# Perceiver layer: the routing between attention and the experts, rewritten around one root, one rank step and a gather by token tiles

## The chip, the cores and the metric

The kernel runs on one core of one Trainium2 chip. The metric is device time in microseconds (us) of one execution. Between changes of this kernel it is the median of several runs.

## The reference

One transformer-like layer over 256 tokens of width 512, in float32, with a context of 25088 rows. It adds three blocks to x, each behind a layernorm: a two-way cross attention with the context, a self-attention with 16 heads, and a feed-forward block with a shared expert and 32 routed ones, of which each token goes to one. Only the last block matters here:

```python
x = x + _L0_ffn_ref(_layernorm(x), gate_w, shared_gate_w, ..., routed_down_w)
# inside, x is the normalized input of 256 tokens:
shared_out = silu(x @ sg) * (x @ su) @ sd
logits = x @ gate_w                            # 32 experts
topk_ids = argmax(logits, -1); topk_val = max(logits, -1)
xs = x * sigmoid(topk_val)[:, None]
order = argsort(topk_ids); sorted_x = xs[order]
g = ragged_dot(sorted_x, routed_gate_w, tokens_per_expert)
u = ragged_dot(sorted_x, routed_up_w, tokens_per_expert)
d = ragged_dot(silu(g) * u, routed_down_w, tokens_per_expert)
return shared_out + d[argsort(order)]
```

Gate, up and down matrices are 512x1024, 512x1024 and 1024x512 for each expert, 2 MB each: 96 matrices, 192 MB (of 2 MB = 2097152 bytes), are read once.

## The kernel before

The 256 tokens are two token tiles (t = 0, 1) of 128 partitions. Matrix products are on TensorE (PE), each product of float32 appearing in the trace as two records; vector work on VectorE (DVE); activations and half of the copies out of PSUM on ScalarE (ACT); transfers are issued by SyncE's queue (SP), in order. The program runs under a tile framework that puts in the waits between engines and may order instructions on an engine; the changed kernel uses its `issue_after` to say behind which instruction another one is to stand.

Stages, by the profile's clock: the cross attention over 49 blocks of 512 context rows until about 690 us, its gate and mix until 724, self-attention until 808, routing until 822, experts until the end. There are 11 slots of 2 MB for weights (`feed`, `done`, lines 118 to 129): a list names the matrices to come in order, and when the last reader of a slot is through, SP may issue the next transfer into it (line 122). At the start of the routing gate (rg), up (ru) and down (rd) of experts 0 to 2 and some more are in the slots or on their way.

Routing, lines 779 to 835, before the change, with the names that the rows use:

- y[t] in PSUM holds the sum behind self-attention (line 745 is its last product). Each tile has statistics (788), mean and variance (184), variance plus eps (ve, 186), a square root on ACT (188), a reciprocal (190) and the normalization into h2: tile 0 on DVE (196), tile 1 on ACT (194).
- Four PE transposes for each tile give h2T (792), copied out by DVE or ACT (101/99). ACT also copies y[t] to x_sb (835), from which a product with the identity opens the output's sum acc[t] (969), written in the loop behind expert 0's products but placed on PE among the transposes.
- Logits lg (798), eight records for each tile; then on DVE the maximum mx (803), a comparison (805), a sum with `far` (807), a minimum that gives the expert's number eid (808), and the one-hot row (809).
- The rank of a token within its expert: products with `before` (a strict triangle) and, for tile 1, with `ones` (817, 818); then a product with the one-hot row, a sum and key = 256*eid + rank (820, 822, 823).
- The score is a sigmoid (829), and h2 is scaled by it on ACT (831).
- `select(g)` (841) compares the keys with the slots of four experts at a time (32 slots for each expert), and `gather_tokens` multiplies h2 with that selection (884): four column chunks c, the two token tiles within each. `spread_keys` (854) puts all keys in every partition, `count_more` (866) counts tokens above 32 for an expert.
- Experts: `expert_up` (902) makes gate and up products, `expert_down` (921, 930) the down products and their sum into acc through a selection. Shared expert work (940, 952) is spread over experts 3 to 12.

Of the kernel before, what the change touches and what calls it, by code (L numbers as in the profile page):

```python
# [48 lines left out]
def perceiver_layer(  # L49
# [45 lines left out]
    def evacuate(dst, src):  # L95

        turn[0] ^= 1
        if turn[0]:
            nc.vector.tensor_copy(dst, src)  # L99
        else:  # L100
            nc.scalar.copy(dst, src)  # L101


    x_sb = keep.tile([P, NT, H], F32, tag="x", name="x_sb")
    nc.sync.dma_start(x_sb, x)
# [22 lines left out]
    def done(name):  # L128
        feed(weights.pop(name)[1])

    def feed_pair(slot, name, src):
# [4 lines left out]
        for k in range(2):  # L136
# [26 lines left out]
    )  # L163
    iota_m = cpool.tile([P, P], F32, tag="iota_m", name="iota_m")
    nc.gpsimd.iota(iota_m, pattern=[[1, P]], base=0, channel_multiplier=0,
                   allow_small_or_imprecise_dtypes=True)

    iota_4 = cpool.tile([P, P], F32, tag="iota_4", name="iota_4")
# [12 lines left out]
    def normalize(dst, src, stats, name, on_scalar=False):  # L181

        mv = small.tile([P, 2], F32, tag="ln_mv", name=f"{name}_mv")
        nc.vector.bn_aggr(mv, stats)
        ve = small.tile([P, 1], F32, tag="ln_ve", name=f"{name}_ve")
        nc.vector.tensor_scalar(ve, mv[:, 1:2], EPS, None, ALU.add)
        sd = small.tile([P, 1], F32, tag="ln_sd", name=f"{name}_sd")
        nc.scalar.activation(sd, ve, AF.Sqrt)
        rs = small.tile([P, 1], F32, tag="ln_rs", name=f"{name}_rs")
        nc.vector.reciprocal(rs, sd)  # L190
        if on_scalar:
            off = small.tile([P, 1], F32, tag="ln_off", name=f"{name}_off")
            nc.vector.tensor_scalar(off, mv[:, 0:1], rs, -1.0, ALU.mult, ALU.mult)
            nc.scalar.activation(dst, src, AF.Identity, bias=off, scale=rs)
        else:
            nc.vector.tensor_scalar(dst, src, mv[:, 0:1], rs, ALU.subtract, ALU.mult)
# [439 lines left out]
    with tc.tile_pool(name="att", bufs=1, reuse_waits="tile") as at:  # L636
# [117 lines left out]
        for hp in range(HC):  # L754
# [10 lines left out]
                att_out(hp - 1, last)  # L765
            pr = following
        att_out(HC - 1, oh)
        done("w_o")
        at_stack.close()

# [11 lines left out]
    eid = fp.tile([P, NT], F32, tag="eid", name="eid")  # L782
    onehot = fp.tile([P, NT, E], F32, tag="onehot", name="onehot")
    far = fp.tile([P, E], F32, tag="far", name="far")
    nc.vector.tensor_scalar(far, iota_m[:, :E], float(E), None, ALU.add)
    for t in range(NT):
        st = small.tile([P, 6], F32, tag="ln_st", name=f"ln2_st{t}")
        nc.vector.bn_stats(st, y[t])
        normalize(h2[:, t, :], y[t], st, f"ln2_{t}", on_scalar=(t == 1))
        pt = tr_bank(f"h2T_{t}")  # L790
        for c in range(KC):
            nc.tensor.transpose(pt[:, ts(c, P)], h2[:, t, ts(c, P)], ident)
        evacuate(h2T[:, :, ts(t, P)], pt.rearrange("p (c n) -> p c n", c=KC))
    mx = fp.tile([P, NT], F32, tag="mx", name="mx")
    for t in range(NT):
        pm = tr_bank(f"lg_{t}")
        for c in range(KC):
            nc.tensor.matmul(
                pm[:, :E], h2T[:, c, ts(t, P)], gw_sb[:, c, :],
                start=(c == 0), stop=(c == KC - 1),  # L800
            )

        nc.vector.tensor_reduce(mx[:, t : t + 1], pm[:, :E], AX.X, ALU.max)
        cand = small.tile([P, E], F32, tag="cand", name=f"cand_{t}")
        nc.vector.tensor_scalar(cand, pm[:, :E], mx[:, t : t + 1], -float(E),
                                ALU.is_equal, ALU.mult)
        nc.vector.tensor_tensor(cand, cand, far, ALU.add)
        nc.vector.tensor_reduce(eid[:, t : t + 1], cand, AX.X, ALU.min)
        nc.vector.tensor_scalar(
            onehot[:, t, :], iota_m[:, :E], eid[:, t : t + 1], None, ALU.is_equal  # L810
        )


    for t in range(NT):
        pm = tr_bank(f"rank_{t}")
        for k in range(t):
            nc.tensor.matmul(pm[:, :E], ones, onehot[:, k, :], start=(k == 0), stop=False)
        nc.tensor.matmul(pm[:, :E], before, onehot[:, t, :], start=(t == 0), stop=True)
        rk = small.tile([P, E], F32, tag="cand", name=f"rk_{t}")
        nc.vector.tensor_tensor(rk, onehot[:, t, :], pm[:, :E], ALU.mult)  # L820
        rank = small.tile([P, 1], F32, tag="rank", name=f"rank_{t}")
        nc.vector.tensor_reduce(rank, rk, AX.X, ALU.add)
        nc.vector.scalar_tensor_tensor(
            key[:, t : t + 1], eid[:, t : t + 1], float(N), rank, ALU.mult, ALU.add
        )


    score_sb = fp.tile([P, NT], F32, tag="score", name="score_sb")
    nc.scalar.activation(score_sb, mx, AF.Sigmoid)
    for t in range(NT):  # L830
        nc.scalar.activation(
            h2[:, t, :], h2[:, t, :], AF.Copy, scale=score_sb[:, t : t + 1]
        )
    for t in range(NT):
        nc.scalar.copy(x_sb[:, t, :], y[t])

    def select(g):

        sl = fp2.tile([P, NT, P], F32, tag="sel", name=f"sel_{g}", bufs=1)
        for t in range(NT):  # L840
            nc.vector.tensor_scalar(
                sl[:, t, :], iota_4, float(4 * N * g), key[:, t : t + 1], ALU.add, ALU.is_equal
            )
        return sl

    keys = fp.tile([P, N], F32, tag="keys", name="keys")

    def spread_keys():

        pm = tr_bank("keys")  # L850
        for t in range(NT):
            dg = fp2.tile([P, P], F32, tag="selT", name=f"dg_{t}")
            nc.vector.tensor_scalar(dg, ident, key[:, t : t + 1], None, ALU.mult)
            nc.tensor.matmul(pm[:, ts(t, P)], ones, dg, start=True, stop=True)
        nc.vector.tensor_copy(keys, pm[:, :N])
# [23 lines left out]
    def gather_tokens(name, sels):  # L879

        pt = tr_bank(f"xg_{name}")
        for c in range(KC):
            for t in range(NT):
                nc.tensor.matmul(
                    pt[:, ts(c, P)], h2[:, t, ts(c, P)], sels[:, t, :],
                    start=(t == 0), stop=(t == NT - 1),
                )
        xg = fp2.tile([P, KC, P], F32, tag="xg", name=f"xg_{name}", bufs=1)
        for half in range(2):
            evacuate(  # L890
                xg[:, 2 * half : 2 * half + 2, :].rearrange("p c m -> p (c m)"),
                pt[:, ts(half, 2 * P)],
            )
        return xg

    def expert_up(name, xg, j, wg_e, wu_e):

# [31 lines left out]
        for t in range(NT):  # L929
            nc.tensor.matmul(accs[t], slT[:, ts(t, P)], d, start=start, stop=stop)  # L930

    acc = [acc_bank(f"acc_{t}") for t in range(NT)]

    def shared_hidden(i):

        w = weight(f"sh_{i // 4}", IC // 2 * P)
# [22 lines left out]
    for e in range(E):  # L959
        wg_e, wu_e = weight(f"rg_{e}", I), weight(f"ru_{e}", I)  # L960
        g, j = divmod(e, 4)
        if j == 0:
            xg = gather_tokens(str(g), select(g))
        act = expert_up(str(e), xg, j, wg_e, wu_e)
        done(f"rg_{e}")
        done(f"ru_{e}")
        if e == 0:
            for t in range(NT):
                nc.tensor.matmul(acc[t], ident, x_sb[:, t, :], start=True, stop=False)

            shT = keep.tile([P, 4, N], F32, tag="x", name="shT")
            spread_keys()
        elif e == 1:
            count_more()
        if pending is not None:
            expert_down(*pending)
            done(f"rd_{e - 1}")
        if 5 <= e < 5 + IC:
            shared_out(e - 5)
        if 3 <= e < 3 + IC:  # L980
            shared_hidden(e - 3)
# [13 lines left out]
    with tc.If(any_more > 0):  # L995
        for s in range(MORE):
# [38 lines left out]
            for t in range(NT):  # L1035
                kr = small.tile([P, 1], F32, tag="o_kr", name=f"o_kr_{s}_{t}")
                nc.vector.tensor_tensor(kr, key[:, t : t + 1], k0, ALU.subtract)
                nc.vector.tensor_scalar(
                    sl[:, t, :CAP], iota_m[:, :CAP], kr, None, ALU.is_equal
                )  # L1040
            xg = gather_tokens(f"o{s}", sl)
# [81 lines left out]
```

## Time and profile before

| | |
|---|---|
| median of 3 runs | 1273.73 us (1271.55 to 1274.98) |
| profiled execution, its time | 1273.0 us |
| its span, first to last instruction | 1271.0 us |
| mean granted TensorE clock | 0.974 |
| busy PE / DVE / ACT / POOL | 1142.1 / 567.3 / 217.4 / 199.2 us |
| read from HBM | 328.82 MB |
| the chain of waits, by engine | PE 70%, DMA 25%, DVE 3%, issue 1%, ACT 1% |

How to read the rows below. A timeline row has the start in us from the span's start, the length, the engine, the line, the operation, output<-inputs and shapes, how many instructions were merged (x), and, in brackets, the idle time of the engine before it and what ended it. A row of a window has the stretch, its length, busy time of PE, PE's weight loads, DVE, ACT and POOL with numbers of instructions, the granted PE clock (1.00 is full speed), the busy share of the DMA engines and GB/s. A row of the chain has start, length, engine, output and line. Ends of matmuls are modelled.

### The profile page before, as it was taken

The page shows a single profiled execution, that of the slowest core. Times are in us where ns is not written, and L with a number is a line of the kernel's source. Part 1 is how long each engine was busy: PE and PEld are TensorE (multiplying, and loading weights), DVE is VectorE, ACT ScalarE, POOL GpSimd, SP SyncE. Part 2 cuts the span into 40 slices and gives each one's busy share as a digit, 9 for nine tenths or more (in the row PEclk, how much of TensorE's full clock was granted, in tenths as well). Part 3 has the DMA queues.
Part 4 walks back from the last instruction along what each step waited for, and adds up shares of the span by engine and source line. Part 5 has one row for each costly group of instructions (what it writes and reads, how often), then busy time and mean ns, then how long its engine had stood idle before and what let it go on. Part 6 is the DMA issues. An engine that isn't in the chain of part 4 may idle for free.

```text
span 1271.0 us, 16289 instructions
## 1 busy us (share of the span) xinstructions
PE 1142.1 (90%) x6732; PEld 833.5 (66%) x6732; DVE 567.3 (45%) x1078; ACT 217.4 (17%) x457; POOL 199.2 (16%) x166
## 2 busy tenths in 40 slices
PE   7999999999999999999999999899998767566665
PEld 6788888888888888888887666554544223222321
DVE  2267766876667866668766445511111010010000
ACT  0222221222211222212221233310001000000000
POOL 1015313333123332133331000000000000000000
PEclk9999999999999999999999999999999898998898
DMA  9554444445444444444441480699999999999996
GB/s 387 228 198 166 166 166 149 163 163 187 151 154 160 166 166 166 166 146 165 163 154 36 181 348 15 259 419 430 430 430 428 430 428 432 429 429 429 429 430 260
DMA packets 30894, 330.44 MB, mean 260 GB/s; under 512 B 3553, under 2 KB 3681, under 8 KB 4065
## 3 DMA queue, kind: packets, MB, share of 16 engines
q1 hardware_dynamic: 30816, 329.36, 65.3%
q8 instruction: 55, 0.90, 0.3%
q14 instruction: 23, 0.18, 0.0%
HBM read 328.82 MB, written 0.52 MB: 259 GB/s over the span
## 4 chain that ended last, share of the span: by engine, by line
PE 70%; DMA 25%; DVE 3%; issue 1%; ACT 1%; POOL 0%; DVEq 0%; ACTq 0%; SPq 0%
PE sc L392 26%; PE p L514 22%; DMA rd<-in_ro_d_dram 9%; DMA rg<-in_ro_g_dram 9%; DMA ru<-in_ro_u_dram 6%; PE d L921 2%; PE rg L902 2%; PE acc L930 2%; PE ru L902 2%; PE y L745 1%; PE vh L654 1%; PE shg L940 1%; PE q L676 1%; PE shu L940 1%; PE k L676 1%
## 5 line engine op out<-in xcount | busy, mean ns | idle before, releaser
L392 PE MATMUL sc<-aT,ctxT 128*128 128x256 f32 x1568 | 341.3, 380 | 0.8 <-DMA ctxT<-in_cxT_dram 0.8
L392 PEld LDWEIGHTS sc<-aT,ctxT 128*128 128x128 f32 x1568 | 298.6, 191 | 40.8 <-ACT st L396 1.1
L514 PE MATMUL p<-diffs,sums 128*128 128x256 f32 x576 | 156.0, 380 | 0.4 <-DVE diffs L480 0.4
L514 PEld LDWEIGHTS p<-diffs,sums 128*128 128x128 f32 x576 | 109.6, 190 | 15.3 <-DVE diffs L480 0.8
L921 PE MATMUL d<-rd,actT 128*32 128x512 f32 x512 | 77.2, 717 | 37.8 <-DMA rd<-in_ro_d_dram 29.5
L396 ACT COPY st<-sc 128x512 f32<-128x512 f32 x98 | 57.3, 585 | 277.7 <-PE sc L392 277.7
L442 POOL TENSOR_TENSOR ls<-ls,st 128x512 f32<-128x512 f32 x64 | 104.2, 1628 | 3.8
L902 PE MATMUL ru<-ru,xg 128*32 128x256 f32 x1024 | 68.7, 407 | 37.8 <-DMA ru<-in_ro_u_dram 37.8
L400 DVE TENSOR_TENSOR mx<-mx,st 128x512 f32<-128x512 f32 x64 | 47.0, 734 | 124.4 <-ACT st L396 124.0
L514 PE MATMUL p<-ctx,st 128*128 128x256 f32 x384 | 98.6, 380 | 0.0
L928 DVE TENSOR_SCALAR selT<-keys,slot_key 128x256 f32<-128x256 f32 x32 | 11.2, 353 | 179.4 <-PE acc L930 179.4
L908 DVE TENSOR_TENSOR act<-act,ru 128x256 f32<-128x256 f32 x32 | 13.5, 421 | 165.7 <-PE ru L902 165.7
L930 PE MATMUL acc<-d,selT 128*128 128x512 f32 x128 | 66.5, 643 | 16.5 <-ACT d L101 16.5
L514 PEld LDWEIGHTS p<-ctx,st 128*128 128x128 f32 x384 | 73.1, 190 | 9.7
L902 PEld LDWEIGHTS ru<-ru,xg 128*32 128x32 f32 x1024 | 32.9, 116 | 70.3 <-DMA ru<-in_ro_u_dram 46.9
L409 POOL PARTITION_ALL_REDUCE mbc<-mx x17 | 18.8, 1104 | 361.1 <-DVE mx L401 353.9
L438 ACT ACTIVATE st<-st 128x512 f32<-128x512 f32 x98 | 59.7, 629 | 77.7 <-DVE m L420 72.7
L902 PE MATMUL rg<-rg,xg 128*32 128x256 f32 x1024 | 64.5, 385 | 1.1 <-DVE xg L99 0.3
L435 DVE TENSOR_TENSOR st<-st,mbc 128x512 f32<-128x512 f32 x98 | 62.7, 688 | 0.0
L921 PEld LDWEIGHTS d<-rd,actT 128*32 128x32 f32 x512 | 17.7, 121 | 67.5 <-issue 55.4
L930 PEld LDWEIGHTS acc<-d,selT 128*128 128x128 f32 x128 | 22.7, 198 | 58.9 <-ACT d L101 42.4
L514 PE MATMUL p<-ctx,sums 128*128 128x256 f32 x192 | 57.3, 380 | 0.4 <-DVE sums L494 0.4
(233 smaller groups left out, 1268.3 us busy)
## 6 DMA issues: line engine op xcount, KB each, us to landing
rg<-in_ro_g_dram SPq DMA_DIRECT2D x32, 2048.0 KB, 37.8
ru<-in_ro_u_dram SPq DMA_DIRECT2D x32, 2048.0 KB, 38.8
rd<-in_ro_d_dram SPq DMA_DIRECT2D x32, 2048.0 KB, 38.9
ctxT<-in_cxT_dram SPq DMA_DIRECT2D x49, 1024.0 KB, 4.9
ctx<-in_cx_dram SPq DMA_DIRECT2D x49, 1024.0 KB, 4.9
sh<-in_sh_gu_dram SPq DMA_DIRECT2D x2, 2048.0 KB, 19.4
w_qc_ks<-in_w_qc_ks_dram SPq DMA_DIRECT2D x2, 1024.0 KB, 6.5
w_kc_qs<-in_w_kc_qs_dram SPq DMA_DIRECT2D x2, 1024.0 KB, 10.8
```

The source lines that it names most:

```text
L392: nc.tensor.matmul(pm[:, ts(u, N)], cols[b][:, c, ts(2 * h + u, P)], aT[:, c, :], start=(c == 0), stop=(c == KC - 1),)
L396: nc.scalar.copy(st[:, i, :], pm)
L400: nc.vector.tensor_tensor(mx, mx, st[:, i, :], ALU.max)
L435: nc.vector.tensor_tensor(pair, pair, mbc.to_broadcast([P, 2, N]), ALU.subtract)
L438: nc.scalar.activation(st[:, i, :], st[:, i, :], AF.Exp, scale=xscale)
L442: nc.gpsimd.tensor_tensor(ls, ls, st[:, i, :], ALU.add)
L514: nc.tensor.matmul(bank[n][:, ts(o, half)], left[:, i, :], right[:, h, :], start=(i == 0 and o == 0), stop=(i == 2 * SPAN - 1 and (o == 1 ...
L676: nc.tensor.matmul(pm[:, :N], w[:, c, ts(hp, P)], h1T[:, c, :], start=(c == 0), stop=(c == KC - 1),)
L902: nc.tensor.matmul(pm[ts(q, CAP), : I // 4], xg[:, c, ts(j, CAP)], w[:, c, ts(q, I // 4)], start=(c == 0), stop=(c == KC - 1),)
L921: nc.tensor.matmul(pd[ts(q, CAP), :], actT[:, k, ts(q, CAP)], wd_e[:, 2 * q + k, :], start=(k == 0), stop=(k == 1),)
L930: nc.tensor.matmul(accs[t], slT[:, ts(t, P)], d, start=start, stop=stop)
L940: nc.tensor.matmul(pm[:, :N], w[:, o + c, ts(i % 4, P)], h2T[:, c, :], start=(c == 0), stop=(c == KC - 1),)
```

## The change

It rewrites the routing, in these parts:

- One root for both token tiles: the variances of both go into one 128x2 tile, with one addition, one square root and one reciprocal.
- The copies of y to x_sb stand behind the normalization (tile 0) and behind the second sigmoid (tile 1). acc[0] is opened behind the logits of tile 1, acc[1] behind the gather of the first four experts.
- The expert's number is kept multiplied by 256 (`iota_e`), and one fused instruction multiplies one-hot and rank, sums, and adds it: the key. DVE's steps of the two tiles stand alternately.
- h2 is not scaled; the sigmoid of each tile goes into the selections as a second operand. Selections of later groups compare with shifted keys `kg`.
- The gather loops over token tiles outside and chunks inside, and the first group's selections are made as soon as each tile's keys are there.
- `spread_keys` stands behind the gather; `count_more` comes later on PE by the built order.
- Fillers: eight products with the identity on PE behind attention's last product, whose result nobody reads.

In the built order SP's transfers are the same and stand in the same order. On ACT, the table load of the square root stands ahead of its wait before the change and behind the wait for ve after it.

```diff
+    def keep_clock(bank, rounds, left, right):
+        for _ in range(rounds):
+            nc.tensor.matmul(
+                bank[: left.shape[1], : right.shape[1]], left, right, start=True, stop=True
+            )
...
+    nc.gpsimd.iota(iota_e, pattern=[[N, E]], base=0, channel_multiplier=0,
...
         att_out(HC - 1, oh)
+        keep_clock(mm_bank("idle_1"), 8, ident, oh[:, :P])
         done("w_o")
...
+    mv = fp.tile([P, NT, 2], F32, tag="mv", name="ln2_mv")
     for t in range(NT):
         st = small.tile([P, 6], F32, tag="ln_st", name=f"ln2_st{t}")
         nc.vector.bn_stats(st, y[t])
-        normalize(h2[:, t, :], y[t], st, f"ln2_{t}", on_scalar=(t == 1))
+        nc.vector.bn_aggr(mv[:, t, :], st)
+    ve = fp.tile([P, NT], F32, tag="ve", name="ln2_ve")
+    nc.vector.tensor_scalar(ve, mv[:, :, 1], EPS, None, ALU.add)
+    sd = fp.tile([P, NT], F32, tag="sd", name="ln2_sd")
+    nc.scalar.activation(sd, ve, AF.Sqrt)
+    rs = fp.tile([P, NT], F32, tag="rs", name="ln2_rs")
+    nc.vector.reciprocal(rs, sd)
...
+    with tc.issue_after(normalized.ins):
+        nc.scalar.copy(x_sb[:, 0, :], y[0])
...
+        scored = nc.scalar.activation(score_sb[:, t : t + 1], mx[:, t : t + 1], AF.Sigmoid)
...
-        nc.vector.tensor_tensor(rk, onehot[:, t, :], pm[:, :E], ALU.mult)
-        rank = small.tile([P, 1], F32, tag="rank", name=f"rank_{t}")
-        nc.vector.tensor_reduce(rank, rk, AX.X, ALU.add)
-        nc.vector.scalar_tensor_tensor(
-            key[:, t : t + 1], eid[:, t : t + 1], float(N), rank, ALU.mult, ALU.add
+        nc.vector.tensor_tensor_reduce(
+            rk, onehot[:, t, :], pm[:, :E], 1.0, eid[:, t : t + 1], ALU.mult, ALU.add,
+            accum_out=key[:, t : t + 1],
         )
-    score_sb = fp.tile([P, NT], F32, tag="score", name="score_sb")
-    nc.scalar.activation(score_sb, mx, AF.Sigmoid)
-    for t in range(NT):
-        nc.scalar.activation(
-            h2[:, t, :], h2[:, t, :], AF.Copy, scale=score_sb[:, t : t + 1]
+    def select_tile(sl, t, keys_of):
+        return nc.vector.tensor_scalar(
+            sl[:, t, :], iota_4, keys_of[:, t : t + 1], score_sb[:, t : t + 1],
+            ALU.is_equal, ALU.mult,
         )
...
+    lgs = [logits(t) for t in range(NT)]
+    with tc.issue_after(lgs[1][1].ins):
+        start_sum(0)
+    scored = [assign(t, lgs[t][0]) for t in range(NT)]
+    with tc.issue_after(scored[1].ins):
+        nc.scalar.copy(x_sb[:, 1, :], y[1])
+    sel_0 = fp2.tile([P, NT, P], F32, tag="sel", name="sel_0", bufs=1)
+    rank(0)
+    chosen = select_tile(sel_0, 0, key)
+    with tc.issue_after(chosen.ins):
+        rank(1)
+    chosen = select_tile(sel_0, 1, key)
...
-        for c in range(KC):
-            for t in range(NT):
-                nc.tensor.matmul(
+        for t in range(NT):
+            for c in range(KC):
+                gathered = nc.tensor.matmul(
                     pt[:, ts(c, P)], h2[:, t, ts(c, P)], sels[:, t, :],
-                    start=(t == 0), stop=(t == NT - 1),
+                    start=(t == 0 and c == 0), stop=(t == NT - 1 and c == KC - 1),
                 )
...
+        if e == 0:
+            with tc.issue_after(gathered.ins), tc.issue_after(chosen.ins):
+                start_sum(1)
+                spread_keys()
         act = expert_up(str(e), xg, j, wg_e, wu_e)
...
         if e == 0:
-            for t in range(NT):
-                nc.tensor.matmul(acc[t], ident, x_sb[:, t, :], start=True, stop=False)
             shT = keep.tile([P, 4, N], F32, tag="x", name="shT")
-            spread_keys()
```

More of the change, by code (lines that the diff above doesn't have):

```diff
@@ L165, in perceiver_layer @@
     nc.gpsimd.iota(iota_m, pattern=[[1, P]], base=0, channel_multiplier=0,
+                   allow_small_or_imprecise_dtypes=True)
+    iota_e = cpool.tile([P, E], F32, tag="iota_e", name="iota_e")
+    nc.gpsimd.iota(iota_e, pattern=[[N, E]], base=0, channel_multiplier=0,
                    allow_small_or_imprecise_dtypes=True)
@@ L784, in perceiver_layer @@
     far = fp.tile([P, E], F32, tag="far", name="far")
-    nc.vector.tensor_scalar(far, iota_m[:, :E], float(E), None, ALU.add)
+    nc.vector.tensor_scalar(far, iota_e, float(N * E), None, ALU.add)
+    mv = fp.tile([P, NT, 2], F32, tag="mv", name="ln2_mv")
     for t in range(NT):
@@ L788, in perceiver_layer @@
         nc.vector.bn_stats(st, y[t])
-        normalize(h2[:, t, :], y[t], st, f"ln2_{t}", on_scalar=(t == 1))
+        nc.vector.bn_aggr(mv[:, t, :], st)
[5 more added lines that the diff above has]
+    nc.vector.reciprocal(rs, sd)
+    off = fp.tile([P, 1], F32, tag="off", name="ln2_off")
+    nc.vector.tensor_scalar(off, mv[:, 1, 0:1], rs[:, 1:2], -1.0, ALU.mult, ALU.mult)
+    normalized = nc.scalar.activation(h2[:, 1, :], y[1], AF.Identity, bias=off, scale=rs[:, 1:2])
+    nc.vector.tensor_scalar(h2[:, 0, :], y[0], mv[:, 0, 0:1], rs[:, 0:1], ALU.subtract, ALU.mult)
+    with tc.issue_after(normalized.ins):
+        nc.scalar.copy(x_sb[:, 0, :], y[0])
+    mx = fp.tile([P, NT], F32, tag="mx", name="mx")
+    lgs = []
+    for t in range(NT):
         pt = tr_bank(f"h2T_{t}")
@@ L792, in perceiver_layer, with logits @@
             nc.tensor.transpose(pt[:, ts(c, P)], h2[:, t, ts(c, P)], ident)
-        evacuate(h2T[:, :, ts(t, P)], pt.rearrange("p (c n) -> p c n", c=KC))
-    mx = fp.tile([P, NT], F32, tag="mx", name="mx")
-    for t in range(NT):
-        pm = tr_bank(f"lg_{t}")
+        turned = h2T[:, :, ts(t, P)], pt.rearrange("p (c n) -> p c n", c=KC)
+        if t == 0:
+            nc.vector.tensor_copy(*turned)
+        else:
+            nc.scalar.copy(*turned)
+    def logits(t):
+        pm = mm_bank(f"lg_{t}")
         for c in range(KC):
-            nc.tensor.matmul(
+            last_one = nc.tensor.matmul(
                 pm[:, :E], h2T[:, c, ts(t, P)], gw_sb[:, c, :],
@@ L801, in perceiver_layer, with assign @@
             )
+        return pm, last_one
+    score_sb = fp.tile([P, NT], F32, tag="score", name="score_sb")
+    def assign(t, pm):
         nc.vector.tensor_reduce(mx[:, t : t + 1], pm[:, :E], AX.X, ALU.max)
+        scored = nc.scalar.activation(score_sb[:, t : t + 1], mx[:, t : t + 1], AF.Sigmoid)
         cand = small.tile([P, E], F32, tag="cand", name=f"cand_{t}")
-        nc.vector.tensor_scalar(cand, pm[:, :E], mx[:, t : t + 1], -float(E),
+        nc.vector.tensor_scalar(cand, pm[:, :E], mx[:, t : t + 1], -float(N * E),
                                 ALU.is_equal, ALU.mult)
@@ L809, in perceiver_layer, with rank @@
         nc.vector.tensor_scalar(
-            onehot[:, t, :], iota_m[:, :E], eid[:, t : t + 1], None, ALU.is_equal
+            onehot[:, t, :], iota_e, eid[:, t : t + 1], None, ALU.is_equal
         )
-    for t in range(NT):
-        pm = tr_bank(f"rank_{t}")
+        return scored
+    def rank(t):
+        pm = mm_bank(f"rank_{t}")
         for k in range(t):
             nc.tensor.matmul(pm[:, :E], ones, onehot[:, k, :], start=(k == 0), stop=False)
-        nc.tensor.matmul(pm[:, :E], before, onehot[:, t, :], start=(t == 0), stop=True)
+        nc.tensor.matmul(
+            pm[:, :E], before, onehot[:, t, :], start=(t == 0), stop=True
+        )
@@ L830, in perceiver_layer @@
-    for t in range(NT):
-        nc.scalar.activation(
-            h2[:, t, :], h2[:, t, :], AF.Copy, scale=score_sb[:, t : t + 1]
-        )
-    for t in range(NT):
-        nc.scalar.copy(x_sb[:, t, :], y[t])
+        nc.vector.tensor_tensor_reduce(
+            rk, onehot[:, t, :], pm[:, :E], 1.0, eid[:, t : t + 1], ALU.mult, ALU.add,
+            accum_out=key[:, t : t + 1],
+        )
+    def select_tile(sl, t, keys_of):
+        return nc.vector.tensor_scalar(
+            sl[:, t, :], iota_4, keys_of[:, t : t + 1], score_sb[:, t : t + 1],
+            ALU.is_equal, ALU.mult,
+        )
@@ L837, in select @@
     def select(g):
         sl = fp2.tile([P, NT, P], F32, tag="sel", name=f"sel_{g}", bufs=1)
+        kg = small.tile([P, NT], F32, tag="kg", name=f"kg_{g}")
+        nc.vector.tensor_scalar(kg, key, -float(4 * N * g), None, ALU.add)
         for t in range(NT):
-            nc.vector.tensor_scalar(
-                sl[:, t, :], iota_4, float(4 * N * g), key[:, t : t + 1], ALU.add, ALU.is_equal
-            )
-        return sl
+            select_tile(sl, t, kg)
+        return sl
+    acc = [acc_bank(f"acc_{t}") for t in range(NT)]
@@ new lines, in start_sum @@
+    def start_sum(t):
+        nc.tensor.matmul(acc[t], ident, x_sb[:, t, :], start=True, stop=False)
+    lgs = [logits(t) for t in range(NT)]
[9 more added lines that the diff above has]
+        rank(1)
@@ L881, in gather_tokens @@
         pt = tr_bank(f"xg_{name}")
-        for c in range(KC):
-            for t in range(NT):
-                nc.tensor.matmul(
+        for t in range(NT):
+            for c in range(KC):
+                gathered = nc.tensor.matmul(
                     pt[:, ts(c, P)], h2[:, t, ts(c, P)], sels[:, t, :],
-                    start=(t == 0), stop=(t == NT - 1),
+                    start=(t == 0 and c == 0), stop=(t == NT - 1 and c == KC - 1),
                 )
@@ L893, in gather_tokens @@
             )
-        return xg
+        return xg, gathered
     def expert_up(name, xg, j, wg_e, wu_e):
@@ L930, in expert_down @@
             nc.tensor.matmul(accs[t], slT[:, ts(t, P)], d, start=start, stop=stop)
-    acc = [acc_bank(f"acc_{t}") for t in range(NT)]
     def shared_hidden(i):
@@ L962, in perceiver_layer @@
         if j == 0:
-            xg = gather_tokens(str(g), select(g))
+            xg, gathered = gather_tokens(str(g), select(g) if g else sel_0)
+        if e == 0:
+            with tc.issue_after(gathered.ins), tc.issue_after(chosen.ins):
+                start_sum(1)
+                spread_keys()
         act = expert_up(str(e), xg, j, wg_e, wu_e)
@@ L967, in perceiver_layer @@
         if e == 0:
-            for t in range(NT):
-                nc.tensor.matmul(acc[t], ident, x_sb[:, t, :], start=True, stop=False)
             shT = keep.tile([P, 4, N], F32, tag="x", name="shT")
-            spread_keys()
         elif e == 1:
@@ L1038, in perceiver_layer @@
                 nc.vector.tensor_scalar(
-                    sl[:, t, :CAP], iota_m[:, :CAP], kr, None, ALU.is_equal
+                    sl[:, t, :CAP], iota_m[:, :CAP], kr, score_sb[:, t : t + 1],
+                    ALU.is_equal, ALU.mult,
                 )
-            xg = gather_tokens(f"o{s}", sl)
+            xg, _ = gather_tokens(f"o{s}", sl)
             act = expert_up(f"o{s}", xg, 0, ws[0], ws[1])
```

## Prediction

> **What bounds the kernel now.** I read the chain of waits first, then the issues of the DMA queue (SP), then windows over the stretch between them, then that stretch's timeline. The chain of waits, in order of time (start, length, what), ends so:
>
> ```profile
> 950.78 1.77 PE ru L902 x32
> 952.57 33.04 DMA rg<-in_ro_g_dram
> 1221.22 38.87 DMA rd<-in_ro_d_dram
> 1260.22 3.34 PE d L921 x16
> ```
>
> From 952 us on the end is a stream of expert weights; PE has only 10.8 us left after the last transfer. The chain names PE before 952, but the windows (length, busy time by engine, granted clock, DMA share, GB/s) tell more:
>
> ```profile
> 819.00:820.00 1.00, 1.00 (x8) 1.00 (x8) 0.93 (x3) 0.00 (x0) 0.00 (x0) 0.66 0.80 344
> 820.00:821.00 1.00, 1.00 (x7) 1.00 (x6) 0.11 (x1) 0.00 (x0) 0.00 (x0) 0.50 0.01 0
> 821.00:822.00 1.00, 1.00 (x7) 1.00 (x6) 0.39 (x1) 0.00 (x0) 0.00 (x0) 0.50 0.00 0
> 822.00:823.00 1.00, 1.00 (x14) 0.61 (x17) 0.73 (x6) 0.91 (x2) 0.00 (x0) 0.63 0.00 0
> 823.00:824.00 1.00, 1.00 (x28) 0.52 (x24) 0.84 (x5) 0.74 (x1) 0.00 (x0) 1.00 0.00 0
> 880.00:890.00 10.00, 8.54 (x55) 4.01 (x57) 1.11 (x3) 0.97 (x2) 0.00 (x0) 1.00 1.01 428
> ```
>
> The DMA engines are empty from 819.8 to about 825, and full at 428 to 430 GB/s from 827 until 1260. They never run dry there: at 873.55, after the longest pause between issues (12 us), about five issued transfers of 4.9 us each were still to come. So the end moves one for one with the first issue that closes the hole, as long as it is pulled in by less than 4.6 us. SP's timeline shows that issue:
>
> ```profile
> 808.82 0.37 SPq L122 DMA_DIRECT2D rg<-in_ro_g_dram  x1
> 824.44 0.33 SPq L122 DMA_DIRECT2D ru<-in_ro_u_dram  x1
> 826.16 0.33 SPq L122 DMA_DIRECT2D rd<-in_ro_d_dram  x1
> ```
>
> The 824.44 issue needs the slot that expert 0's gate products (rg) read last. Hence one number decides: when rg of expert 0 ends. From the end of attention's last product (y, 808.35 = 806.37 + 1.98) to 824.44 are 16.1 us, all routing:
>
> ```profile
> 804.71 1.28 ACT L188 ACT_TABLE_LOAD   x1
> 809.68 0.20 ACT L188 ACTIVATE ln_sd<-ln_ve 128x1 f32<-128x1 f32 x1 [0.81 <-DVE ln_ve L186]
> 810.00 0.79 DVE L196 TENSOR_SCALAR h<-y,ln_mv,ln_rs 128x512 f32<-128x512 f32 x1
> 813.67 1.10 PE L969 MATMUL acc<-x_sb,ident 128*128 128x512 f32 x2
> 815.63 0.19 DVE L803 TENSOR_REDUCE mx<-lg 128x1 f32<-128x32 f32 x1 [0.55 <-PE lg L798]
> 817.97 0.28 DVE L841 TENSOR_SCALAR sel<-iota,key 128x128 f32<-128x128 f32 x1
> 818.83 2.75 PE L884 MATMUL xg<-sel,h 128*128 128x128 f32 x14
> 822.20 2.17 PE L902 MATMUL rg<-rg,xg 128*32 128x256 f32 x32
> ```
>
> The first row is the one to remember: the square root's table is loaded at 804.71, in idle time, 4 us before its input is there.
>
> **The change, part by part,** on the clock of this execution (1273.0 us, span 1271.0; 0.7 under the median 1273.73, inside the runs' spread of 3.4).
>
> *One root.* The built order of the changed kernel puts ACT's wait for the variances **in front of** the table load, since this root carries two waits. Stats of tile 1 can start at 808.39, and by the old steps (0.73 to the aggregate, 0.1 for tile 0's between, 0.21 to ve, 0.19 to ACT) ACT is free at 809.65, like 809.68 before. Then come 1.28 of loading and 0.02 (at 713.37 a load was followed by its activation 1.30 later): root at 810.95, 1.27 late. The saved second root and reciprocal were not the last wait. By the Trainium skill, page "ScalarE: Activation LUTs", section "What ACT_TABLE_LOAD costs", a switch also drains about 1.38 us behind the 1.283 us load; this trace shows no drain in the 1.30, and by the page everything below would be 1.4 later. Reciprocal (0.24), offset (0.2), 0.11: tile 0's normalization at 811.5 against 810.00.
>
> *Start of the sums moved off PE's path.* Before, a 0.9 to 1.1 us product (acc) and its copies on ACT stood ahead of tile 1's transposes and of its logits. Now transposes start at 812.44 (0.94 behind normalization, as before), both tiles back to back; copy at 813.10 (0.66 later), logits (lg) at 813.95, 16 records at 0.107 plus 0.17 of latency: tile 1's maximum (mx) at about 815.9 against 815.63. So what the table load costs (1.3 to 1.5), leaving acc out nearly repays: **+0.27**.
>
> *Rank and key in one step.* Old: maximum to tile 1's selection 2.34 us, three DVE steps (817.33, 817.55, 817.77) between rank and selection. New: one fused multiply-reduce; its nearest row, attention's 128-column one, takes 0.21 to its accumulator read and 0.08 for that, so 0.64 becomes about 0.4. But both tiles' steps now alternate on DVE, tile 0's one-hot comes 0.5 later, and rank 0, `ones` and rank 1 (6 records, 0.12 each) queue together on PE: +0.15 to 0.25. Bounds -0.25 to +0.25; I take 0, the old row. Tile 1's selection at 818.24, tile 0's about 0.6 earlier. acc of tile 0 (0.94) ends as rank 0 becomes ready, 0.9 after the maximum: hidden at full clock, 0.8 exposed at half.
>
> *Scores inside the selections* take two scaling activations (0.71 each) off ACT. Before, they held the gather to 818.83 together with the keys; that wait goes. The scores' table load runs behind tile 1's copy and beside the logits, sigmoid done 0.7 after the maximum, selection 1.75 after it: nothing.
>
> *Gather by token tiles.* Tile 0's eight records run from 818.05 (0.40 behind its selection), tile 1's follow without a hole: 16 records at 0.112 to 0.122 (a later gather, at 853.24, took 1.95) end at 820.0, against 821.58: **-1.6**.
>
> *Products behind it.* Tile 1's sum start (two records, 0.43 each) and four records of keys (0.45) now stand between the gather and rg on PE. rg would have waited 0.5 to 0.6 for xg's copy anyway (855.19 to 855.71 there); it starts at about 821.2, 0.7 later than it could; before: 822.20. Then 1.97 to the issue (824.19 to 826.16 for ru): **823.2 against 824.44, -1.25** at full clock. Counting moves behind expert 1's products, 0.5 us while the stream has transfers waiting: nothing. The seven subtractions for later selections (kg, about 0.15 on DVE each): nothing.
>
> *Fillers.* Eight products of 128 columns, 16 records, 1.7 to 2.0 us, PE 808.35 to 810.3; the transposes come at 812.44, so nothing waits on PE. They read oh, whose space feeds the slot issued at 808.82; held until 810.3, that transfer still stands behind the 4.9 us one of 808.38. SP's order of issues is unchanged.
>
> *The clock.* In the windows above it is at half speed from 819.32 to 822.74, 3.42 us (0.68 + 1 + 1 + 0.74), and so it was once earlier, 723.74 to 727.16, again 3.42, and 28 times 3.414 before. In the first it cost the gather 1.2 (2.75 for 14 records against 1.57) and rg 0.24: 1.4 in all. Each stood behind some 3.4 us in which PE did little. Fillers end at 810.3, but then PE is idle for 2.1 us, and transposes and logits of 32 columns until 815.8 keep it little used, more than one such stretch. So I expect one half-speed stretch on the path still, earlier than before. It can cost 1.71 at most; before it cost 1.4, and over logits and ranks part is hidden: 1.1. **Sum: -1.25 + 1.1 = -0.15**, ends -1.25 and +0.46. The Trainium skill, "TensorE: Matmul & The Clock Gate", Part 1, speaks of a free-running window of 3413 ns, which the trace bears out; its Part 4 adds that transposes don't count as busy, which no row here isolates and which would work against the fillers.
>
> **The rivals.** (1) *The fillers hold the clock* through the gather: for it, at 812.5 and 815.9 the old kernel kept full speed after windows little busier than these; against it, the 5.6 us above. -1.25: 1272.5. (2) *Slower: two half-speed stretches in a row.* If a window begins near 809, both it and the next are sparse, and logits, tile 0's acc, ranks and half the gather run at half clock: -1.25 + 2.7 = +1.4, 1275.1. It decides if a boundary of the 3.4 us windows falls within about 0.6 us of 812.5, so that a whole sparse one lies on either side. (3) *The change doesn't do what it says*: as to the root, this is in my main case, where the load eats the saving; were the load early all the same, 1.3 less, 1272.2. (4) Something in the stream itself; 3.8 us either way would need 0.9% of its 430 us, and no part of the change touches it.
>
> **How the numbers follow.** Main case 0.55: 1273.73 - 0.15, about 1273.5. Rival (1) 0.25, rival (2) 0.15, rival (3)'s early load and the rest 0.05. A measurement of this kernel tells about 0.3% (3.8 us) from no change; all named cases lie within it. Range: from rival (1) less its unknowns (0.3) and half the spread (1.7), 1270.5, to rival (2) plus 0.9, 1276.0. Faster by over 0.3% 0.03, within 0.94, slower 0.03.
>
> **What would show it.** Right: a table load that starts at about 809.6 and its root 1.3 later; the second maximum within 0.5 of 815.6; two halves of the gather without a gap; acc and keys directly ahead of rg; the closing issue between 823 and 825; a full stream as before. Wrong: a table load before 808 (then -1.3 more), a half-speed stretch on gather and products, an issue outside 822.5 to 826, or a stream that isn't at 428 to 430 GB/s.

## The result, and the profile after

The changed kernel takes 1277.31 us (median of 11 runs, 1275.24 to 1280.53) against 1273.73 of the kernel before (11 runs): ratio 1.0035, 95% interval 1.0021 to 1.0048. It is a little slower: by 0.35% as the ratio has it (4.5 us; the interval is 2.7 to 6.1) and by 3.6 us, 0.28%, between the medians. That is about the 0.3% that the prediction had named as the least that can be told from no change, and the median lies above its range, which ended at 1276.0. The profiled execution took 1275.24 us, its span is 1273.5.

The chain of waits of the changed kernel ends as that of before did, in a stream of weights (start, length, what):

```profile
951.75 1.77 PE ru L959 x32
953.54 34.78 DMA rg<-in_ro_g_dram
1225.22 39.07 DMA rd<-in_ro_d_dram
1264.42 1.96 PE d L978 x16
```

The last rd is issued at 1225.22 against 1221.22: 4.0 us later. SP's timeline splits them:

```profile
807.62 0.33 SPq L130 DMA_DIRECT2D sh<-in_sh_gu_dram  x1
808.06 0.37 SPq L130 DMA_DIRECT2D rg<-in_ro_g_dram  x1
826.57 0.33 SPq L130 DMA_DIRECT2D ru<-in_ro_u_dram  x1
828.29 0.33 SPq L130 DMA_DIRECT2D rd<-in_ro_d_dram  x1
```

The first row is issued when attention's last product is through (before: 808.38), the third is the issue that closes the hole in the stream (before: 824.44). Below, **path** is the time from the first to the third, and **stream** the time from the third to the last rd issue.

| | before | after | |
|---|---|---|---|
| attention's end | 808.38 | 807.62 | -0.76 |
| path | 16.06 | 18.95 | +2.89 |
| stream | 396.78 | 398.65 | +1.87 |
| from the last rd issue to the span's end | 49.78 | 48.28 | -1.50 |
| span | 1271.0 | 1273.5 | +2.5 |

So two things were lost, not one. The gain of 1.50 in the row before the last isn't the change's: the last down products (d, at the end of the chains) take 3.34 us at half clock in the trace of the kernel before and 1.96 at full clock in this one. Over the traces of all 14 kernels that row lies between 48.1 and 52.7 us, and attention's end between 806.1 and 811.0. So single times differ by some us for reasons outside the routing, and path and stream are read apart.

The path first; the timeline of the changed kernel (start, length, what; brackets: idle before and its end):

```profile
807.43 1.95 PE L107 MATMUL idle<-oh,ident 128*128 128x128 f32 x16
...
808.84 1.28 ACT L807 ACT_TABLE_LOAD   x1 [4.91 <-DVE ln_ve L805]
810.14 0.20 ACT L807 ACTIVATE ln_sd<-ln_ve 128x2 f32<-128x2 f32 x1
...
811.65 1.07 PE L822 MATMUL h2T<-ident,h 128*128 128x128 f32 x8 [2.27 <-DVE h L813]
...
813.07 3.62 PE L831 MATMUL lg<-gw_sb,h2T 128*128 128x32 f32 x16 [0.35 <-DVE h2T L825]
...
819.72 3.62 PE L941 MATMUL xg<-sel,h 128*128 128x128 f32 x16
...
823.17 1.02 PE L887 MATMUL acc<-x_sb,ident 128*128 128x512 f32 x2
...
824.03 0.61 PE L910 MATMUL keys<-dg,ones 128*128 128x128 f32 x4
...
824.57 1.93 PE L959 MATMUL rg<-rg,xg 128*32 128x256 f32 x32
```

The order is the expected one, with the table load behind ACT's wait, but logits and gather take 3.62 us each, about twice what they should. Windows of the changed kernel, cut where the granted clock changes (length, busy PE, PE's weight loads, DVE, ACT, POOL, clock, DMA share, GB/s), and its full stream at the end, show why:

```profile
809.41:812.82 3.41, 1.07 (x8) 0.86 (x8) 1.60 (x4) 2.24 (x5) 0.00 (x0) 1.00 0.92 380
812.82:816.23 3.41, 3.16 (x15) 3.16 (x16) 0.64 (x3) 2.01 (x3) 0.00 (x0) 0.50 0.99 423
816.23:819.64 3.41, 3.41 (x11) 2.23 (x10) 1.79 (x11) 0.68 (x2) 0.00 (x0) 0.50 0.84 360
819.64:823.06 3.42, 3.38 (x17) 3.37 (x17) 1.28 (x9) 0.00 (x0) 0.00 (x0) 0.50 0.00 0
823.06:826.47 3.41, 3.41 (x44) 2.11 (x47) 2.15 (x7) 1.66 (x2) 0.00 (x0) 1.00 0.02 5
...
960.00:1200.00 240.00, 166.45 (x1500) 68.71 (x1500) 23.29 (x61) 17.60 (x37) 0.00 (x0) 0.90 1.01 427
```

The first window begins where the fillers end and holds a gap and the transposes: PE is busy 1.07 of 3.41 us; three windows at half clock follow, 10.24 us against 3.42 before, over logits, ranks and gather. And the stream runs at 427 GB/s; the same 240 us of the kernel before have 429.

### The profile page after: what moved, and what is told of

Its sections match the earlier page's. It is cut to its first block, busy times and chain, and to the rows that moved or that the text cites. A ratio compares the mean times of both kernels' runs of the same rounds, so it can differ in the third digit from the quotient of the medians.

```text
span 1273.5 us, 16325 instructions
## 1 busy us (share of the span) xinstructions
PE 1148.4 (90%) x6748; PEld 836.5 (66%) x6748; DVE 568.3 (45%) x1081; ACT 216.4 (17%) x455; POOL 199.2 (16%) x167
## 4 chain that ended last, share of the span: by engine, by line
PE 71%; DMA 25%; DVE 2%; issue 1%; ACT 1%; POOL 0%; DVEq 0%; ACTq 0%; SPq 0%
PE sc L404 26%; PE p L526 22%; DMA rd<-in_ro_d_dram 9%; DMA rg<-in_ro_g_dram 9%; DMA ru<-in_ro_u_dram 6%; PE d L978 2%; PE rg L959 2%; PE acc L987 2%; PE ru L959 2%; PE y L757 1%; PE vh L666 1%; PE shg L995 1%; PE q L688 1%; PE shu L995 1%; PE k L688 1%
```

## The experiments

All times are medians; a ratio is to runs of the kernel before beside them on the same chip, whose median lay between 1272.8 and 1273.8, so that it isn't quite the quotient of two times in the table; "half clock" is what the profiled execution shows between attention's end and the closing issue.

| kernel | time, us | ratio, 95% interval | path | half clock | stream |
|---|---|---|---|---|---|
| before | 1273.73 | | 16.06 | 3.42 | 396.78 |
| after | 1277.31 | 1.0035 [1.0021, 1.0048] | 18.95 | 10.24 | 398.65 |
| e1 early load | 1271.59 | 0.9997 [0.9982, 1.0012] | 13.63 | 0 | 398.86 |
| e2 long fillers | 1272.31 | 0.9999 [0.9986, 1.0012] | 16.60 | 3.42 | 398.48 |
| e3 sums early | 1276.76 | 1.0026 [1.0009, 1.0043] | 15.32 | 0 | 398.65 |
| e4 before, sums late | 1274.31 | 1.0008 [0.9994, 1.0021] | 19.83 | 13.66 | 396.90 |
| e5 slots back | 1275.41 | 1.0011 [0.9996, 1.0027] | 18.94 | 10.24 | 396.97 |
| e6 before, slots shifted | 1276.45 | 1.0007 [0.9987, 1.0027] | 19.68 | 13.66 | 398.66 |
| e7 early load, slots back | 1269.03 | 0.9965 [0.9947, 0.9983] | 13.64 | 0 | 397.01 |
| e8 all slots at 512 | 1267.39 | 0.9950 [0.9934, 0.9966] | 13.64 | 0 | 395.67 |
| e9 no fillers | 1276.78 | 1.0037 [1.0022, 1.0051] | 18.96 | 10.24 | 396.81 |
| e10 products behind rg | 1267.75 | 0.9968 [0.9953, 0.9984] | 12.92 | 0 | 396.89 |
| e11 all repairs | 1267.91 | 0.9962 [0.9948, 0.9976] | 12.93 | 0 | 395.79 |
| e12 before, fillers | 1269.90 | 0.9983 [0.9971, 0.9995] | 14.54 | 0 | 396.91 |

**e1, the table load ahead of the wait.** The root's result goes into another pool, so that its instruction carries one wait:

```diff
-    sd = fp.tile([P, NT], F32, tag="sd", name="ln2_sd")
+    sd = small.tile([P, NT], F32, tag="ln_sd2", name="ln2_sd")
```

> The changed kernel with the square root's output in another pool, so that its table load is ready ahead of the wait again; nothing else. Number to read: the routing path, from the end of attention's last product to the issue that closes the stream's hole (16.09 us before, 18.98 after). Theory clock (three half-speed windows cost 4.1 us, because PE has too little to do between the fillers and the gather): the path gets 1.3 us shorter by the load, and PE's idle time between fillers and transposes falls from 2.2 to 1.0 us, which may save a half-speed window as well: 14.5 to 17.7. Theory load (the load on the path is what cost): 17.7 and as many half-speed windows as after. Theory stream (the weights come slower, 426 to 428 GB/s against 428 to 430, by something in the change): path shorter, time as after (ratio 1.0035).

```profile
803.47 1.28 ACT L807 ACT_TABLE_LOAD   x1
```

The load is in idle time again, and the root starts at 808.31, 1.17 us behind attention's end. The load by itself costs 1.28 us, but the path got 5.3 us shorter, and the ratio fell from 1.0035 to 0.9997, some 5 us. With the root earlier, PE's gap before the transposes shrinks and no window of this trace goes to half clock. The stream stayed at 398.86, though the routing was 5 us shorter: its loss doesn't come from there. (The edit isn't quite alone: the new small tile has four buffers, and by the sizes of the pools they move the six younger weight slots by 128 bytes. The stream doesn't show it.)

**e2, fillers that reach up to the transposes.**

```diff
-        keep_clock(mm_bank("idle_1"), 8, ident, oh[:, :P])
+        keep_clock(mm_bank("idle_1"), 17, ident, oh[:, :P])
```

> The changed kernel with 17 fillers in place of 8, which end just before the transposes can start (about 811.4 against 811.6); nothing else. Theory clock: the window before the logits is busy, at most one half-speed window remains, the path falls from 18.98 to 14.9 to 16.6 us, ratio to the kernel before about 1.000. Theory load: the path stays at 19, or 0.2 above if the fillers run into the transposes, ratio 1.0035. Theory stream: path shorter, ratio as after.

They take 3.96 us (34 records). The late root stays, yet 4.6 us of the loss are back by the ratios (1.0035 to 0.9999): what the late root costs is mainly the gap that it opens, and these fillers close it. One window at half clock remained, on the gather (3.64 us).

**e3, the sums' start among the logits, as before the change.**

```diff
-        nc.scalar.copy(x_sb[:, 0, :], y[0])
+        for t in range(NT):
+            nc.scalar.copy(x_sb[:, t, :], y[t])
...
-    lgs = [logits(t) for t in range(NT)]
-    with tc.issue_after(lgs[1][1].ins):
-        start_sum(0)
+    start_sum(0)
+    lgs = [logits(0)]
+    with tc.issue_after(lgs[0][1].ins):
+        start_sum(1)
+        lgs.append(logits(1))
     scored = [assign(t, lgs[t][0]) for t in range(NT)]
-    with tc.issue_after(scored[1].ins):
-        nc.scalar.copy(x_sb[:, 1, :], y[1])
...
-                start_sum(1)
                 spread_keys()
```

> The changed kernel with the two openings of the sums back where the kernel before had them, acc 0 ahead of tile 0's logits and acc 1 between the two tiles' logits; load and fillers as in the changed kernel. Theory clock: these dense products kept the clock up; at most one half-speed window, and for 0.5 to 1.4 us that they hold up the logits the path is 16 to 17.5 us instead of 18.98. Theory load: they only hold up the logits, path 19 to 20.4.

**e4, the converse: the kernel before with the first sum behind the logits, the second behind the gather.**

```diff
...
+    acc = [acc_bank(f"acc_{t}") for t in range(NT)]
+    with tc.issue_after(last_lg.ins):
+        nc.tensor.matmul(acc[0], ident, x_sb[:, 0, :], start=True, stop=False)
...
+        if e == 0:
+            with tc.issue_after(gathered[0].ins):
+                nc.tensor.matmul(acc[1], ident, x_sb[:, 1, :], start=True, stop=False)
```

> The kernel before with one part of the change alone: acc 0 opened behind the logits of tile 1, acc 1 behind the gather. Theory clock: two or three half-speed windows in a row where there was one, path 17 to 19 us against 16.09, ratio 1.001 to 1.002. Theory load: no clock change, logits 0.9 us earlier, acc 1 ahead of the gate products 0.4 later, path 15.2 to 16, ratio 0.9995.

The two profiles (no half clock in e3, four windows in e4) look as if the place of these two products decided the clock. The times don't bear it out: e3 is at 1276.76, its interval overlaps that of the changed kernel, and e4 can't be told from the kernel before. e6 then showed four windows in the old order itself. A single profile is one draw of the windows' phase, that is, of where their borders fall; the theory that the sums had kept the clock isn't supported.

**e5, the slots back where they were.** The new constant is 128 bytes a partition. Among the constants it pushes the pool of the five oldest weight slots from byte 20480 (a multiple of 512) to 20608 in the built program. Here it stands behind x_sb instead:

```diff
-    iota_e = cpool.tile([P, E], F32, tag="iota_e", name="iota_e")
+    iota_e = keep.tile([P, E], F32, tag="iota_e", name="iota_e")
```

> The changed kernel, with its one new constant (iota_e, 128 bytes a partition) taken out of the pool of constants and put behind x_sb, so that the five oldest weight slots begin at byte 20480 of a partition again (a multiple of 512) and not at 20608; every other address and every instruction stays. Theory PLACE (the 1.9 us that the stream lost come from where the slots begin): closing issue to last rd issue back from 398.65 to about 396.8 us, 429 GB/s in 960 to 1200; routing as in the changed kernel, 18 to 19 us from y to the closing issue (up to two 3.4 us windows less if the phase of the clock falls well); time about 1275.3, ratio 1.0012. Rival CLOCK (the stream is slower because of what the routing does, or of the chip's state): 398.65 us and 427 GB/s as before this edit, time 1277.3.

**e6, the kernel before with its slots shifted and nothing else.**

```diff
+    spare = cpool.tile([P, E], F32, tag="spare", name="spare")
+    nc.gpsimd.memset(spare, 0.0)
     iota_m = cpool.tile([P, P], F32, tag="iota_m", name="iota_m")
```

> The kernel before, with nothing of the change but 128 more bytes a partition in the pool of constants (one memset tile that nothing reads), so that all weight slots begin 128 bytes later: the five oldest at 20608 and on. PLACE: closing issue to last rd issue 396.8 to about 398.7 us, 427 GB/s; routing as before (16 us); time about 1275.5, ratio 1.0015. CLOCK, or anything else in the change: 396.8 us, 429 GB/s, ratio 1.000.

The stretch of full stream, 960 to 1200 us, of e5 and then of e6 (columns as above, the last is GB/s):

```profile
960.00:1200.00 240.00, 166.21 (x1516) 68.35 (x1516) 23.72 (x63) 17.98 (x38) 0.00 (x0) 0.91 1.01 429
```

```profile
960.00:1200.00 240.00, 168.46 (x1508) 69.28 (x1500) 22.79 (x61) 17.96 (x38) 0.00 (x0) 0.89 1.01 427
```

It follows the place of the slots in both directions: 396.97 us with e5, 398.66 with e6, each within 0.2 of what was expected. e5's path stayed at 18.94. e6's times don't settle it (1.0007, with an interval of 0.4%); its traces do. e6 is also the old routing at another phase of the clock; its windows:

```profile
807.07:810.48 3.41, 1.35 (x6) 0.85 (x7) 2.45 (x8) 1.67 (x4) 0.00 (x0) 1.00 0.86 269
810.48:813.89 3.41, 3.41 (x14) 2.90 (x13) 0.45 (x3) 2.14 (x3) 0.00 (x0) 0.50 1.02 437
813.89:817.31 3.42, 3.29 (x12) 2.38 (x10) 1.10 (x6) 0.26 (x2) 0.00 (x0) 0.50 0.98 422
817.31:820.72 3.41, 3.16 (x12) 2.73 (x13) 2.10 (x13) 1.28 (x2) 0.00 (x0) 0.50 0.24 101
820.72:824.14 3.42, 3.42 (x18) 3.42 (x17) 1.45 (x4) 0.00 (x0) 0.00 (x0) 0.50 0.00 0
```

A window with PE busy for 1.35 us, then four at half clock, and a path of 19.68. In the trace of the kernel before, the window at nearly the same place read as follows, and stayed at full clock:

```profile
809.08:812.49 3.41, 1.55 (x7) 0.92 (x8) 2.25 (x8) 1.87 (x4) 0.00 (x0) 1.00 0.99 312
```

So the 16.06 us of the old path were one draw as well. The 12 times of e6 lie in two groups, 1270.6 to 1272.5 (5) and 1276.4 to 1281.0 (7), as such a draw would make them; the mean granted clock of the first group is 0.974 to 0.980, that of the second 0.966 to 0.972. Which windows of the slower executions were at half clock isn't on record, except for the one that was profiled, which took 1276.43.

**e7, e1 and e5 together.**

> The changed kernel with both repairs: the root's table loaded ahead of its wait (as in e1) and the new constant behind x_sb (as in e5). If the causes add up: path from y to the closing issue 13.6 to 14 us (e1: 13.63), closing issue to last rd issue 396.8 (PLACE) or 398.8 (CLOCK). Time by PLACE 1269.7 (e1's 1271.6 less 1.9), ratio 0.997 and faster than both kernels; by CLOCK 1271.6, ratio 0.9985.

```profile
812.13 0.20 ACT L807 ACTIVATE ln_sd<-ln_ve 128x2 f32<-128x2 f32 x1 [3.57 <-DVE ln_ve L805]
...
815.05 1.97 PE L831 MATMUL lg<-gw_sb,h2T 128*128 128x32 f32 x16 [0.35 <-DVE h2T L825]
...
819.34 2.02 PE L941 MATMUL xg<-sel,h 128*128 128x128 f32 x16 [0.45 <-DVE sel L869]
821.20 1.02 PE L887 MATMUL acc<-x_sb,ident 128*128 128x512 f32 x2
...
822.60 1.93 PE L959 MATMUL rg<-rg,xg 128*32 128x256 f32 x32
824.59 0.33 SPq L130 DMA_DIRECT2D ru<-in_ro_u_dram  x1
```

In this timeline of e7 logits and gather take 1.97 and 2.02 us, not 3.62. The repairs add up, and e7 is faster than both kernels, by 0.35% (0.17 to 0.53) against the one before.

**e8, all eleven slots at multiples of 512 bytes.** The six younger slots begin at 320 beyond one in the kernels before and after. On top of e5's edit, four small tiles get one buffer instead of four (one is shown), 64 bytes are added, and the root goes into a small tile that exists (so that its load is early, as in e1):

```diff
+    spare = keep.tile([P, 16], F32, tag="spare", name="spare")
+    nc.gpsimd.memset(spare, 0.0)
...
-    sd = fp.tile([P, NT], F32, tag="sd", name="ln2_sd")
+    sd = small.tile([P, NT], F32, tag="kg", name="ln2_sd")
...
-            col = small.tile([P, 1], F32, tag="o_col", name=f"o_col_{s}")
+            col = small.tile([P, 1], F32, tag="o_col", name=f"o_col_{s}", bufs=1)
```

> As e7, and the six younger slots (five of the late pool, one of the last) moved as well so that all eleven begin at a multiple of 512 bytes; before they begin at 320 beyond one. If each transfer into a slot at a multiple of 512 is some 0.05 us shorter (1.9 us over about 36 transfers of the 80 of the stream), the other 44 give about 2.3 us more: closing issue to last rd issue about 394.5, about 431 to 432 GB/s, time 1267.4, ratio 0.995. If only the five oldest slots matter, or a multiple of 128 is not what counts: 396.8 and time as e7.

The stream fell by another 1.3 us, to 395.67, at 430 GB/s; 2.3 had been expected. With none, five and eleven slots in place it takes 398.7, 396.9 and 395.7: the six younger ones bring less than the five. Why, these runs don't tell. With 1267.39 us, e8 has the lowest median of all, though its interval overlaps that of e7.

**e9, no fillers, on e5.**

```diff
-        keep_clock(mm_bank("idle_1"), 8, ident, oh[:, :P])
```

> The changed kernel with the old slot addresses (e5) and without the eight fillers behind attention; the late root stays. Theory CLOCK (what remains of the loss, 1.6 us by e5, is half-speed windows in a routing made sparse by the late root): the sparse window before the transposes gets emptier, so three or four half-speed windows (10.2 to 13.7 us) on the path at nearly every phase of the clock, path 19 to 20 us, time 1276 to 1277.5 against e5's 1275.4. Rival ORDER (the new order on PE itself costs it, and the fillers do nothing): 1275.4, path as e5, or shorter where fillers delayed the transposes.

The ratio rose from 1.0011 to 1.0037, some 3 us, though the two intervals touch: the fillers of the change seem to do their part. The profile doesn't show it: its windows happened to be cut 1.78 us behind attention's end, as in e5 and the changed kernel, where the fillers (1.95 us) lie ahead of the sparse window.

**e10, tile 1's sum and the keys behind rg, on e7; e11, the same on e8 with 12 fillers.**

```diff
-        if e == 0:
-            with tc.issue_after(gathered.ins), tc.issue_after(chosen.ins):
-                start_sum(1)
-                spread_keys()
...
+            with tc.issue_after(last_up[0].ins):
+                start_sum(1)
+                spread_keys()
             shT = keep.tile([P, 4, N], F32, tag="x", name="shT")
```

> As e7 (early load, slots back), with tile 1's start of the sum and the products of keys put behind expert 0's gate and up products again, where the old kernel had them. If they cost what the prediction said (0.7 us ahead of rg, none of it hidden): path from y to the closing issue 13.64 to 12.9, time 1268.3 against e7's 1269.0. If they are hidden by xg's copy, or if rg then waits for something else: 13.6, 1269.0.

> Candidate best: as e8 (early load, all eleven slots at multiples of 512 bytes), 12 fillers instead of 8 so that they reach up to the transposes, and the sum's start and keys behind expert 0's products as in e10. Path 12.9 us, no half-speed window before the closing issue, closing issue to last rd issue 395.7; time 1266.6, ratio 0.9945. If the fillers delay the transposes or the keys are missed later: as e8, 1267.4, or above.

The path falls from 13.64 to 12.92, as expected. In the time it doesn't show: e7, e10, e8 and e11 have overlapping intervals, and e11 missed its 1266.6.

**e12, the kernel before with the eight fillers alone.**

> The kernel before with the eight fillers alone. CLOCK: the old routing too goes to half speed at some phases of the clock (16.06 us with one window in the kernel before's trace, 19.68 with four in e6's); fillers keep the first window dense at more phases, path 14.7 to 16, time 1272 to 1272.5, ratio 0.999. ORDER (the phases don't matter to the time): 1273.8.

The path is 14.54 without half clock, and the time falls by 0.17% (about 2 us), the interval clear of 1. The edit is that of the change's `keep_clock`, at the same place. So the old routing lost some 2 us to the clock on average (0.6 to 3.7 by the interval, and more if fillers don't hold the clock in every execution), and the fillers were worth having by themselves.

## Why the prediction was wrong

**What bounds the end: right.** The closing issue decides, and the stream behind it never runs dry in any of the 14 traces.

**The parts at full clock: right, nearly to the tenth.** Counted from attention's end, the root started at 2.52 (predicted 2.57), transposes at 4.03 (4.06), logits at 5.45 (5.57). e7 shows the rest at full clock, 1.27 earlier for its early load: gather at 8.39, so 9.66 with the late one (9.67), and a path of 13.64 + 1.27 = 14.91 (823.2 - 808.38 = 14.8). The two products ahead of rg cost 0.72 (e10; 0.7), and a full-speed old path 14.54 (e12; 16.06 - 1.4 = 14.66). What the text didn't draw out of its own numbers: against the *old path at full clock* the change is no gain but 14.91 - 14.54 = +0.4. Its -1.25 came from the old kernel's half-speed window (1.4) and nothing else.

**The clock term: the first step that failed.** "One half-speed stretch on the path still", at 1.1 us, became three windows and 18.95 - 14.91 = 4.0 us in the profiled execution. Rival (2) had the mechanism and the sign, but stopped at two windows; its condition, a boundary near 812.5, isn't needed either, as the sparse window ran from 1.79 behind attention's end. The signs that the text had named for being wrong came: half clock on the gather, an issue 18.95 us behind attention's end (827.3 on the prediction's clock), a stream at 427.

The text went by stretches "in which PE did little". Ahead of the old half-speed window that wasn't so:

```profile
815.91:819.32 3.41, 2.40 (x15) 1.96 (x16) 2.61 (x15) 1.48 (x3) 0.00 (x0) 1.00 1.00 428
```

PE was busy 2.40 of 3.41 us there, and 3.33 in the window before it, which stayed at full clock and which the text called little busier than the sparse ones of the new routing. What sorts the windows better stands in the last section.

Two more things were missing. A half-speed window doesn't only slow the work in it: three or four followed each other, though PE was busy 2.84 to 3.41 of 3.41 us in them. And the one window of the kernel before was taken as its fixed price, though the phase differs from execution to execution: over the 14 traces a border fell 0.1 to 3.0 us behind attention's end, and 0.70 in the kernel before against 0.49 in e6 went with 16.06 and 19.68 us in the same routing. What had to be compared is the mean: about 2 us for the old kernel (e12), and for the changed one the 5 to 6 us that an early load brings (e1; e7 against e5), less its 1.3. The late root is thus the main cause on the path: 1.3 by itself, which the prediction had, and 3.5 to 4.5 by the gap that it opens, for which the prediction had 1.1.

**The stream: the second step that failed.** Rival (4) put it aside, at nothing, since "no part of the change touches it". The new constant does, by 128 bytes of address. By e5 and e6 that is all of the 1.87 us, about two fifths of the 4.5 us that the ratio shows. The Trainium skill, page "DMA: Bandwidth & Descriptors", section "How a descriptor splits into AXI transactions", says that a transaction must begin at an address that is a multiple of 256 bytes, and that of a descriptor beginning elsewhere the first transaction starts at the multiple below it, and the bytes before the descriptor's start are fetched unused and still cost; it words this for reads. The slots at 128, 320 and 448 bytes beyond a multiple of 512 all miss such an address, and the runs agree in direction: 398.65 against 395.67 us, 0.75%. Whether a multiple of 256 would do as well as one of 512 was not tried.

**The sum.** In the profiled executions the path's -1.15 at full clock (14.91 less 16.06), 4.04 by the clock and 1.87 in the stream make 4.76 us. Over many executions, of 3.6 us between the medians or 4.5 by the ratio, the stream has 1.9; 0.4 is the longer path at full clock, and the rest, 1.3 to 2.2, is about what the clock's means differ by (3.5 to 4.5 against 2, each uncertain by 1 to 2).

## What to carry to other kernels

Where a stretch of small dependent steps follows dense products, cost it at full clock for both kernels first, and then the clock as a mean over the phases of its window; one profile shows one draw, and a 1.3 us wait can cost 5 if its gap leaves a window with little to stream. When a change adds a constant or a buffer, look at what it moves in memory: the start address of every large DMA target belongs to the change. An instruction with two waits may lose its early table load; a different home for its output gave it back.

## What the runs showed of the hardware

- A stream of 2 MB transfers from HBM runs at 427 GB/s into slots that begin at 128 to 448 bytes beyond a multiple of 512 (the changed kernel, e1, e2, e3, e6), at 429 with five of eleven at such a multiple (before, e4, e5, e7, e9, e10, e12), and at 430 with all (e8, e11).
- Half-speed stretches on the path came in whole windows of 3.41 us, one to four in a row. The share of a window in which PE is busy doesn't decide: those at 0.20 to 0.40 (e4, the changed kernel, e5, e9, e6) were followed by half clock and those at 0.44 to 0.47 (e3, before, e9) not, but a window at 0.70 in the kernel before and one at 0.84 in e2 were followed by half clock too, and so were, ahead of the routing at 720 us, one at 0.44 (before) and one at 0.47 (the changed kernel).
- What decides better is how many columns PE's products stream in a window (the second number of a record's output shape; 256 take 380 ns at full clock on line 392 of the kernel before and 512 take 593 on line 745, so a window has room for some 4100, and for half of that at half clock). This count was worked out from the 14 traces afterwards, and no run was made to test it. Of 494 windows from 715 to 835 us, all 21 with fewer than 1400 columns were followed by half clock, whichever clock they ran at, and none of the 468 with more than 1550; the five between went both ways. It also fits the rows of several windows at half clock: the one at 812.82 of the changed kernel, full of logits of 32 columns, has about 430, the next 1280, the third 1800, and behind that the clock returned. The kernel before had about 1420 in its sparse window and stayed at full clock, e6 had 1270 and didn't. Transposes have to be counted: without them the window at 809.29 of e10 would have 660 of its 1680, and full clock followed.
- The Trainium skill, "TensorE: Matmul & The Clock Gate", Part 1, gives about 3.4 us of busy time for the return to full clock; here windows with PE busy for 2.84 (e4) to 3.41 us, at half clock, were followed by another at half clock.
